# A hybrid of convolution, scan, attention and experts: the first chunk of layer 2 prepared in one go, its second keys put behind the first piece

## The chip, the cores and the metric

The kernel runs on one core of a Trainium2 chip. A core has five engines with queues of their own: PE (matmuls), ACT (functions of one operand), DVE (vector work), POOL (a second, slower vector engine) and SP (which issues DMAs here). Each works through its instructions in order and waits for semaphores. The metric is the device time of one launch in microseconds; less is better.

## What is computed

Four layers over four images of 56 x 56 positions with 128 channels. Layer 0 is neighbourhood attention, layer 1 a two-layer selective scan, layer 2 additive attention and an expert stage, layer 3 softmax attention and a second expert stage. The change lies at the start of layer 2's attention, which is, per image (3136 tokens after a layer norm, 16 hidden units):

```python
f = jnp.einsum('bih,ha->bia', x, W1[:h])
g = jnp.einsum('bjh,ha->bja', x, W1[h:])
t = jnp.tanh(f[:, :, None, :] + g[:, None, :, :] + b1)
scores = jnp.einsum('bija,a->bij', t, w2[:, 0]) + b2[0]
flag = jnp.tril(jnp.ones((n_seq, n_seq), dtype=x.dtype), -1)[None, :, :]
e = jnp.exp(scores) * flag
w = e / (jnp.sum(e, axis=-1, keepdims=True) + 1e-10)
return jnp.einsum('bij,bjh->bih', w, x)
```

Every pair of a query and an earlier key costs 16 tangents.

## The kernel before, in words

**Tiling.** A token tile has 112 tokens (`TP`), an image 28 of them (`NT`). Queries are taken in chunks of seven tiles (`WT`), 784 columns. On the 128 partitions lie eight keys (`JG`) times 16 hidden units, so a key tile has 14 groups of eight keys (`NG`). `fT` holds a chunk's query term (128 x 784; the 16 units eight times below each other), `g` the key term, one column of it for each group of eight keys.

**Pieces.** A piece is half a key tile against a chunk of queries: seven slots of up to 784 columns in one tile `th` (three buffers). In the first chunk of an image every key tile meets only the queries behind it, so the pieces of that chunk shrink: 784, 728, 672, 616, ... 56 columns for each slot; the next chunk begins at 784 again. A piece goes through four steps:
- `adds` (L1297, DVE): seven instructions, each `fT` plus one column of `g`.
- `tangents` (L1306, ACT): one tanh in place over all seven slots.
- `scores` (L1320, PE): `place` (a 0/1 matrix scaled by `w2`) sums the 16 units; four groups of columns of the array work at once. The result lies in one of two PSUM tiles `s`.
- every second piece: `weights` (L1334 or L1337, ACT exponential; on the diagonal a mask L1341 on POOL) and `weighted` (L1350, PE) with the keys' rows `xk`.

The loop over the pieces is a schedule written out by hand: DVE's adds run two pieces ahead of ACT's tangents, the exponential of a key tile comes three pieces behind, its weighted sum four. A list of small steps (`now`, `later_on`, `behind`) is dealt into the loop; from piece 2 on it holds the preparation of the next chunk.

**Preparing a chunk** (`chunk_steps`) is done in two parts, four token tiles and then three. For each part: the norm on DVE (L1221, into `xa`), transposes on PE (L1230), a copy out of PSUM on DVE (L1233, into `xT`), a memset on POOL (L1237) and eight DMAs (L1244) that bring `xa` into the order of `xk`, the key term (L1253 on PE: eight matmuls, two instructions each; L1261 on DVE adds `b1`), and the query term (L1271 on PE; L1275 on DVE copies it into `fT`). All PSUM results of it go through one bank `m`; `xa` and `xT` have one buffer each.

**The start of layer 2.** For the first chunk of the first image there is nothing to lie beside: its steps run straight behind layer 1. The weights `wf` and `wg` (L1379, L1380) and the scaling of `place` (L1381) are made on DVE after the first transposes. Only then come the adds of pieces 0 and 1 and the loop.

**The end of layer 1.** The layer norm of image 0 for layer 2 needs means and variances: 28 pairs of instructions on DVE (L1131, L1132) and a root (`rstd`, L179 to L187, with a Sqrt on ACT at L181). Image 0 has long been complete there; 20 of the pairs are put ahead of the last step of layer 1 on DVE (L920, the residual of the last image, which waits for the matmuls L904), eight and the root behind it.

Of the kernel before, what the change touches and what calls it, by code (L numbers as in the profile page):

```python
# [11 lines left out]
AF = mybir.ActivationFunctionType  # L12
ALU = mybir.AluOpType
# [5 lines left out]
B, HW, C = 4, 56, 128  # L19
S = HW * HW  # L20
P = 128
TP = 2 * HW
NT = S // TP
TC = 4
CH = TC * TP
# [30 lines left out]
AH = 16  # L56
JG = P // AH
NG = TP // JG
QW = 32

WT = 7
# [77 lines left out]
class Hybrid:  # L139
# [612 lines left out]
    def layer1(self):  # L752
# [3 lines left out]
        nc, a, tc = self.nc, self.a, self.tc  # L756
        ET = mybir.EngineType
        with ExitStack() as ctx:
            w = self.w1
            big = ctx.enter_context(tc.tile_pool(name="l1_big", bufs=1, reuse_waits="tile"))  # L760
            sm = ctx.enter_context(tc.tile_pool(name="l1_sm", bufs=2, reuse_waits="tile"))
# [6 lines left out]
            m = lambda: self.t(ps_m, [P, 512], "m")  # L768
# [7 lines left out]
            n_pairs = PAIRS * len(order)  # L776
# [147 lines left out]
            po, first, last = {}, {}, {}  # L924
            add = lambda to, at, f, *args: to.setdefault(at, []).append(lambda: f(*args))
            for j, block in enumerate(order):
                at = PAIRS * j
                if j and block[1:] == (0, 0):

                    g = self.group_norm(block[0], big, w["group"])  # L930
# [9 lines left out]
                    to = at - 2 * PAIRS  # L940
# [16 lines left out]
            g = self.first_norm  # L957
# [4 lines left out]
                turned = lambda c=c: (g.turn(c, m), g.scaled(c, g.ps))  # L962
                add(last, (-4, 2, 10, 12, PAIRS + 2, PAIRS + 10)[c - 1], turned)
            for n, step in enumerate(self.first_stats()):
                add(first if n < 20 else last, n_pairs if n < 20 else n_pairs + 10, step)
            for p in range(-4, n_pairs + PAIRS):
                if inside(p + 1):
                    in_place(p + 1)
# [170 lines left out]
    def layer2_attention(self):  # L1139
# [3 lines left out]
        nc, a, tc = self.nc, self.a, self.tc  # L1143
        ET = mybir.EngineType
        with ExitStack() as ctx:
            wp = ctx.enter_context(tc.tile_pool(name="l2_w", bufs=1, reuse_waits="tile"))
            W1, b1, w2, b2, place, later, back = self.l2

            wf = self.t(wp, [P, JG, AH], "wf")
            wg = self.t(wp, [P, 2 * P - AH], "wg")  # L1150

            big = ctx.enter_context(tc.tile_pool(name="l2_big", bufs=1, reuse_waits="tile"))
            sm = ctx.enter_context(tc.tile_pool(name="l2_sm", bufs=2, reuse_waits="tile"))
            ps_m = ctx.enter_context(tc.tile_pool(name="l2_m", bufs=1, reuse_waits="tile", space=PSUM))
            ps_h = ctx.enter_context(tc.tile_pool(name="l2_h", bufs=1, reuse_waits="tile", space=PSUM))
            ps_s = ctx.enter_context(tc.tile_pool(name="l2_s", bufs=2, reuse_waits="tile", space=PSUM))
            ps_o = ctx.enter_context(tc.tile_pool(name="l2_o", bufs=1, reuse_waits="tile", space=PSUM))
# [3 lines left out]
            m = lambda: self.t(ps_m, [P, 512], "m")  # L1161
            hold = lambda: self.t(ps_h, [P, 512], "h")
# [3 lines left out]
            im, fT, po, ps, th, es = {}, {}, {}, {}, {}, {}  # L1166
            g, xk = {}, {}
# [11 lines left out]
            def span(j, J, half=0):  # L1179

                t, n = chunks[order[j][1]]
                return max(J - t, 0) * TP + (half * TP // 2 if J >= t else 0), n * TP
# [4 lines left out]
            def image_steps(b):  # L1187

                r = im[b] = self.l2_first if b == 0 else {}
                if b == 0:  # L1190
                    return []
                x = self.X[b]

                def stats(t0):
                    if t0 == 0:
                        r["mv"] = self.t(sm, [TP, NT, 2], "ln_mv", bufs=1)
                    for t in range(t0, t0 + 2):
                        st = self.t(sm, [TP, nc.vector.BN_STATS_DIM], "ln_st", bufs=4)
                        nc.vector.bn_stats(st, x[:, t, :])
                        nc.vector.bn_aggr(r["mv"][:, t, :], st)  # L1200

                def root():
                    r["r"] = self.rstd(sm, r["mv"][:, :, 1], [TP, NT], 1e-5, "li", bufs=1)

                return [bind(stats, t) for t in range(0, NT, 2)] + [root]
# [84 lines left out]
            def adds(i):  # L1290
                j, J, half = pieces[i]
                lo, hi = span(j, J, half)
                b = order[j][0]
                th[i] = self.t(sm, [P, NG // 2, WT * TP], "th", bufs=3)
                for s, (blk, q) in enumerate(sum(rounds(half), [])):
                    at = NG * (J % WT) + NG // 2 * half + 2 * blk + (q % 2 if blk < 3 else 0)
                    nc.vector.tensor_scalar(  # L1297
                        th[i][:, s, lo:hi], fT[j][:, lo:hi], g[b, J // WT][:, at : at + 1],
                        None, op0=ALU.add,
                    )  # L1300

            def tangents(i):
                j, J, half = pieces[i]
                lo, hi = span(j, J, half)
                own = th[i][:, :, lo:hi]
                nc.scalar.activation(own, own, AF.Tanh)  # L1306
# [49 lines left out]
            def attended(j):  # L1356
# [13 lines left out]

                return [bind(copied, h) for h in range(2)], [bind(added, s) for s in range(0, n, 2)]

            run = lambda step: (step() or (lambda: None))()
            nc.gpsimd.memset(wg, 0.0)
            image_steps(0)
            start = chunk_steps(0)
            for step in start[:3]:
                run(step)
            nc.vector.tensor_copy(wf, W1[:, 0:1, :].to_broadcast([P, JG, AH]))  # L1379
            nc.vector.tensor_copy(wg[:, P - AH : P], W1[:, 1, :])  # L1380
            nc.vector.tensor_scalar(place, place, w2, None, op0=ALU.mult)  # L1381
            for step in start[3:]:
                run(step)
            weights2 = lambda: setattr(self, "w2", self.experts2_weights(self.f2_w, m))
            urgent, now, later_on, behind = [], [], [], []
            state = SimpleNamespace(held=False, after=lambda: None, dealt=0, credit=0)
            first = {}
# [3 lines left out]
            def add_ahead(i):  # L1391
                if i < len(pieces):
                    j = pieces[i][0]
                    if i == first[j] and j:
                        while now or later_on:
                            assert not state.held
                            run((now or later_on).pop(0))
                    adds(i)


            def deal():
                state.after()
                state.dealt += 1
                step = None
                if urgent and not state.held:
                    step = urgent.pop(0)
                elif now and not state.held:
                    step = now.pop(0)
                elif later_on and state.dealt % 2 and not state.held:
                    step = later_on.pop(0)  # L1410
                elif behind:
                    step = behind.pop(0)
                    state.held = step.holds
                state.after = (step and step()) or (lambda: None)
# [8 lines left out]
            def choose(b):  # L1423

                behind.extend(self.choose_steps(
                    b - 1, self.f2_pooled[:, :, b - 1], self.w2, pools, root
                ))
                if b == B - 1:
                    behind.extend(self.experts2_steps(
                        range(B - 1), self.f2_pooled, self.w2, pools, 2.5, lambda: None  # L1430
                    ))

            add_ahead(0)
            add_ahead(1)
            for i, (j, J, half) in enumerate(pieces):
                tangents(i)
                b, k = order[j]
                if half == 0 and J == 1 and k + 1 < len(chunks):
                    now += chunk_steps(j + 1)
                    if j == 0:  # L1440
                        now.append(weights2)
                if half == 0 and J == 8 and k + 1 == len(chunks) and b + 1 < B:
                    assert not behind
                    later_on += image_steps(b + 1) + chunk_steps(j + 1)
                if b and half == 0 and (k, J) == ((0, 2) if b == B - 1 else (1, 0)):
                    choose(b)
                lo, hi = span(j, J, half)
                state.credit = min(state.credit + SHARE * (hi - lo) / (WT * TP), 2)
                may = [state.credit >= n for n in (1, 2)]
                state.credit -= sum(may)  # L1450
                if may[0]:
                    deal()
                add_ahead(i + 2)
                if i >= 4 and half == 0:
                    gather(*pieces[i - 4][:2])
                scores(i)
                state.after()
                state.after = lambda: None
                if i >= 3 and half == 1:
                    weights(*pieces[i - 3][:2])  # L1460
                if may[1]:
                    deal()
            state.after()
            j, J, _ = pieces[-1]
# [742 lines left out]
```

## Time and profile before

| | us |
|---|---|
| median of 3 runs | 7028.35 (7022.07 to 7032.54) |
| profiled execution | 7027.59 |
| its span | 7025.8 |
| PE, DVE, ACT, POOL busy | 6054.1, 5763.3, 4832.9, 2849.9 |
| mean granted PE clock | 0.931 |
| last step of layer 1 on DVE (L920) starts | 2979.29 |
| first norm of layer 2 (L1221) starts | 2984.91 |
| first add (L1297) starts | 3002.85 |
| first tanh (L1306) starts | 3008.15 |
| last tanh starts | 5599.1 |

The profile shows one execution. All times in it are microseconds from the start of its span. Its views used below: the timeline (instructions of an engine in order of time; in square brackets the time that the engine stood idle ahead of one and what ended that), the groups by line, the chain of waits that ended last, and a table of busy times by stage with the granted PE clock.

### The profile page before, as it was taken

The page shows a single profiled execution, that of the slowest core. Times are in us where ns is not written, and L with a number is a line of the kernel's source. Part 1 is how long each engine was busy: PE and PEld are TensorE (multiplying, and loading weights), DVE is VectorE, ACT ScalarE, POOL GpSimd, SP SyncE. Part 2 cuts the span into 40 slices and gives each one's busy share as a digit, 9 for nine tenths or more (in the row PEclk, how much of TensorE's full clock was granted, in tenths as well). Part 3 has the DMA queues.
Part 4 walks back from the last instruction along what each step waited for, and adds up shares of the span by engine and source line. Part 5 has one row for each costly group of instructions (what it writes and reads, how often), then busy time and mean ns, then how long its engine had stood idle before and what let it go on. Part 6 is the DMA issues. An engine that isn't in the chain of part 4 may idle for free.

```text
span 7025.8 us, 101491 instructions
## 1 busy us (share of the span) xinstructions
PE 6054.1 (86%) x37386; PEld 2622.7 (37%) x37386; DVE 5763.3 (82%) x10108; ACT 4832.9 (69%) x4828; POOL 2849.9 (41%) x1921
## 2 busy tenths in 40 slices
PE   8889999999999999877777777777788799999998
PEld 7633333333233233232233323332333355555554
DVE  6879999999999999977878888888887753566665
ACT  5567667776766777589989998999899833322231
POOL 2369989998999999811010001000101100000000
PEclk9989989999999899889999999999899999999999
DMA  3057767777776777600000000000003304243433
GB/s 53 5 139 187 187 165 186 184 178 175 188 185 171 176 189 187 153 8 3 1 6 3 8 2 6 4 6 3 6 20 116 89 18 149 72 109 92 118 85 94
DMA packets 363447, 654.19 MB, mean 93 GB/s; under 512 B 95413, under 2 KB 211909, under 8 KB 362438
## 3 DMA queue, kind: packets, MB, share of 16 engines
q1 hardware_dynamic: 362949, 647.71, 36.9%
q8 instruction: 295, 4.83, 0.3%
q14 instruction: 203, 1.66, 0.1%
HBM read 536.78 MB, written 104.37 MB: 91 GB/s over the span
## 4 chain that ended last, share of the span: by engine, by line
PE 23%; ACT 12%; DVE 11%; issue 8%; POOL 1%; SPq 0%; DMA 0%; DVEq 0%; ACTq 0%; POOLq 0%
ACT th L1306 10%; PE o L1944 6%; DVE th L1297 6%; PE q L1932 5%; PE s L1320 5%; DVE X L2144 2%; PE pe L2139 2%; ACT e L1334 1%; POOL e L1341 1%; PE o L1350 1%; PE m L1478 1%; PE m L1253 1%; DVE wide L1964 1%; DVE X L1486 0%; PE m L1761 0%
## 5 line engine op out<-in xcount | busy, mean ns | idle before, releaser
L1306 ACT ACTIVATE th<-th 128x5488 f32<-128x5488 f32 (+13 forms) x560 | 2184.2, 3943 | 175.4 <-DVE th L1297 151.4
L1297 DVE TENSOR_SCALAR th<-fT,g 128x784 f32<-128x784 f32 (+13 forms) x3920 | 1868.9, 549 | 307.2 <-PE s L1320 286.5
L1320 PE MATMUL s<-th,place 128*32 128x392 f32 (+5 forms) x14112 | 1391.6, 488 | 442.2 <-ACT th L1306 439.5
L860 DVE TENSOR_TENSOR_SCAN hs<-E,u 128x896 f32<-128x896 f32 x728 | 1449.7, 2007 | 3.6 <-ACT E L844 3.6
L844 ACT ACTIVATE E<-E,rate 128x448 f32<-128x448 f32 x1456 | 886.0, 661 | 121.9 <-DMA E<-delta_dram 118.4
L865 POOL TENSOR_TENSOR hs<-hs,room 128x896 f32<-128x896 f32 x448 | 924.8, 2083 | 82.9 <-DVE hs L860 82.5
L865 POOL TENSOR_TENSOR hs<-hs,bc 128x896 f32<-128x896 f32 x448 | 926.5, 2087 | 47.3 <-DVE hs L860 45.6
L1320 PEld LDWEIGHTS s<-th,place 128*32 128x32 f32 (+1 forms) x14112 | 455.1, 111 | 1311.1 <-ACT th L1306 666.3
L1937 ACT ACTIVATE e<-q,shift 128x448 f32<-128x448 f32 (+1 forms) x511 | 322.0, 633 | 673.7 <-PE q L1932 653.4
L1341 POOL TENSOR_TENSOR e<-e,later 112x112 f32<-112x112 f32 x112 | 155.0, 1384 | 1131.4 <-ACT e L1334 676.6
L2144 DVE SCALAR_TENSOR_TENSOR X<-pe,r_gate,X 112x128 f32<-112x128 f32 x896 | 311.9, 348 | 309.6 <-PE pe L2139 273.5
L871 PE MATMUL y<-hs,sum 128*32 128x448 f32 x3584 | 499.4, 631 | 4.0 <-POOL hs L865 4.0
L1932 PE MATMUL q<-xT 128*128 128x448 f32 (+1 forms) x1022 | 501.3, 573 | 0.9 <-ACT e L1937 0.9
L1944 PE MATMUL o<-e,xk 128*128 128x448 f32 (+1 forms) x1022 | 479.2, 552 | 16.1 <-ACT oT L1909 16.1
L806 PE MATMUL u<-room,pick 32*128 32x448 f32 x1456 | 413.4, 638 | 68.5 <-DVE hs L860 66.7
L1350 PE MATMUL o<-e,xk 112*128 112x392 f32 (+5 forms) x1024 | 389.3, 500 | 91.8 <-POOL e L1341 88.2
L806 PE MATMUL u<-du,pick 32*128 32x448 f32 x1456 | 402.8, 618 | 74.2 <-DVE hs L860 72.9
L1237 POOL MEMSET xa<- 112x4 f32 (+1 forms) x32 | 55.1, 1723 | 969.9 <-PE m L1230 969.8
L853 DVE TENSOR_TENSOR u<-u,bc 128x896 f32<-128x896 f32 x364 | 391.8, 1076 | 26.1 <-PE u L806 25.8
L853 DVE TENSOR_TENSOR u<-u,room 128x896 f32<-128x896 f32 x364 | 391.8, 1076 | 22.0 <-PE u L806 21.9
L2073 POOL MEMSET lc_xa<- 112x4 f32 x28 | 3.1, 109 | 945.7 <-DVE lc_xa L2067 696.4
L848 ACT ACTIVATE u<-u 128x896 f32<-128x896 f32 x168 | 151.9, 904 | 297.3 <-PE u L797 218.1
(310 smaller groups left out, 8767.5 us busy)
## 6 DMA issues: line engine op xcount, KB each, us to landing
E<-delta_dram SPq DMA_DIRECT2D x728, 448.0 KB
V<-du_dram SPq DMA_DIRECT2D x168, 448.0 KB
wide<-in_L_ffn_weight SPq DMA_DIRECT2D x64, 1024.0 KB
r<-M SPq DMA_DIRECT2D x189, 224.0 KB
M<-wide SPq DMA_DIRECT2D x72, 392.0 KB
du_dram<-room SPq DMA_DIRECT2D x112, 112.0 KB
delta_dram<-room SPq DMA_DIRECT2D x112, 112.0 KB
du_dram<-du SPq DMA_DIRECT2D x112, 112.0 KB
```

The lines of the kernel that those rows point to most:

```text
L806: nc.tensor.matmul(halves(to)[:, k], w["pick"][own, q, :], pre[j]["du"][own, f], start=True, stop=True,)
L844: nc.scalar.activation(e, e, AF.Exp, scale=rate)
L853: eng.tensor_mul(v, v, pre[p // PAIRS]["bc"][:, 0:1].to_broadcast([P, 2, CH]))
L860: nc.vector.tensor_tensor_scan(flat, E.pop(p), V.pop(p), 0.0, op0=ALU.mult, op1=ALU.add)
L865: nc.gpsimd.tensor_mul(HS[p], HS[p], bc[:, 1:2].to_broadcast([P, 2, CH]))
L871: nc.tensor.matmul(py[j, f][r * HD : (r + 1) * HD, :], w["sum"][:, q, :], HS[p + r // 2][:, r % 2], start=False, stop=(q == QG - 1),)
L1297: nc.vector.tensor_scalar(th[i][:, s, lo:hi], fT[j][:, lo:hi], g[b, J // WT][:, at : at + 1], None, op0=ALU.add,)
L1306: nc.scalar.activation(own, own, AF.Tanh)
L1320: nc.tensor.matmul(ps[j, J][QW * blk : QW * blk + rows, h, lo:hi], place[:, off : off + rows], z[:, at + s, h * HALF + lo : h * HALF + hi] ...
L1350: nc.tensor.matmul(po[j][:, h, lo:hi], xk[b, J // WT][:, J % WT, :], e[:, h * HALF + lo : h * HALF + hi], start=(J == 0), stop=(J == t + ( ...
L1932: nc.tensor.matmul(ps[:n, :CH], of_tile(xT[b], t), xT[b][:, c * CH : (c + 1) * CH], start=True, stop=True,)
L1944: nc.tensor.matmul(po[b, c], xk[b][:n, t, :], e[:n], start=first, stop=last)
```

## The change

The first chunk is no longer prepared by `chunk_steps` but by a function of its own, `first_chunk`, with `first_keys` behind it for the memsets and DMAs:
- All seven norms follow each other on DVE, with an `xa` of its own for each part (the second in the buffer of `oT`) and an `xT` of its own (the second in a buffer of `fT`). `wf` and `wg` are made ahead of the norms, `place` is scaled behind them.
- The results go through six PSUM banks: `m` and `hold` for the transposes, the two of `o` for the queries, the two of the first `s` for the keys.
- `xT` and `fT` are copied out of PSUM by ACT instead of DVE.
- On PE the order is: transposes of both parts, keys of part 0, queries of part 0, queries of part 1. The keys of part 1 are returned as `later_keys`.
- A tanh of one column (`warm`) is issued on ACT first of all.
- The tangents of piece 0 are seven instructions, one for each slot, issued right behind its adds; `later_keys` follows, and then the adds of piece 1.
- 24 of the 28 pairs of statistics instead of 20 stand ahead of the last step of layer 1.

```diff
-                add(first if n < 20 else last, n_pairs if n < 20 else n_pairs + 10, step)
+                add(first if n < 24 else last, n_pairs if n < 24 else n_pairs + 10, step)
...
+            def first_chunk():
+
+                parts = (0, TC), (TC, WT)
+                r = im[0]
+                warm = self.t(wp, [P, 1], "warm")
+                nc.scalar.activation(warm, b1, AF.Tanh)
+                xT = [self.t(big, [P, CH], "xT"), self.t(sm, [P, WT * TP], "fT")]
+                fT[0] = self.t(sm, [P, WT * TP], "fT")
+                xk[0, 0] = self.t(big, [TP, WT, C], "xk0")
+                g[0, 0] = self.t(big, [P, WT * NG], "g0")
+                xa = [
+                    self.t(big, [TP, TC, C], "xa"),
+                    self.t(sm, [P, WT * TP], "oT", bufs=1)[:TP, : TC * C].rearrange("p (k c) -> p k c", c=C),
+                ]
+                room_q, room_k = self.t(ps_o, [P, 2, 512], "o"), self.t(ps_s, [P, 2, 512], "s")
+                nc.vector.tensor_copy(wf, W1[:, 0:1, :].to_broadcast([P, JG, AH]))
+                nc.vector.tensor_copy(wg[:, P - AH : P], W1[:, 1, :])
+                for n, (t0, t1) in enumerate(parts):
+                    ps = (m, hold)[n]()
+                    for t in range(t0, t1):
+                        nc.vector.tensor_scalar(
+                            xa[n][:, t - t0, :], self.X[0][:, t, :], r["mv"][:, t, 0:1],
+                            r["r"][:, t : t + 1], op0=ALU.subtract, op1=ALU.mult,
+                        )
+                        nc.tensor.transpose(
+                            ps[:, (t - t0) * TP : (t - t0 + 1) * TP], xa[n][:, t - t0, :],
+                            self.ident[:TP, :TP],
+                        )
+                    nc.scalar.copy(xT[n][:, : (t1 - t0) * TP], ps[:, : (t1 - t0) * TP])
+                nc.vector.tensor_scalar(place, place, w2, None, op0=ALU.mult)
+
+                def keys(n, t0, t1):
+                    ps = room_k[:, n, : (t1 - t0) * NG]
+                    by_key = xT[n][:, : (t1 - t0) * TP].rearrange("p (g j) -> p g j", j=JG)
+                    for i in range(JG):
+                        nc.tensor.matmul(
+                            ps, wg[:, P - AH - i * AH : 2 * P - AH - i * AH], by_key[:, :, i],
+                            start=(i == 0), stop=(i == JG - 1),
+                        )
+                    nc.vector.tensor_scalar(g[0, 0][:, t0 * NG : t1 * NG], ps, b1, None, op0=ALU.add)
+
+                keys(0, *parts[0])
+                for n, (t0, t1) in enumerate(parts):
+                    ps = room_q[:, n, : (t1 - t0) * TP]
+                    nc.tensor.matmul(
+                        ps, wf.rearrange("p j a -> p (j a)"), xT[n][:, : (t1 - t0) * TP],
+                        start=True, stop=True,
+                    )
+                    nc.scalar.copy(fT[0][:, t0 * TP : t1 * TP], ps)
+                return xa, parts, lambda: keys(1, *parts[1])
+
+            def first_keys(xa, parts):
+                for n, (t0, t1) in enumerate(parts):
+                    nc.gpsimd.memset(xa[n][:, : t1 - t0, C - 1 : C], 1.0)
...
-            start = chunk_steps(0)
-            for step in start[:3]:
-                run(step)
-            nc.vector.tensor_copy(wf, W1[:, 0:1, :].to_broadcast([P, JG, AH]))
-            nc.vector.tensor_copy(wg[:, P - AH : P], W1[:, 1, :])
-            nc.vector.tensor_scalar(place, place, w2, None, op0=ALU.mult)
-            for step in start[3:]:
-                run(step)
+            xa, parts, later_keys = first_chunk()
+            first_keys(xa, parts)
...
             add_ahead(0)
+            for s in range(NG // 2):
+                nc.scalar.activation(th[0][:, s, :], th[0][:, s, :], AF.Tanh)
+            later_keys()
             add_ahead(1)
             for i, (j, J, half) in enumerate(pieces):
-                tangents(i)
+                if i:
+                    tangents(i)
```

The rest of `first_keys`, left out, is the loop of eight DMAs for each part, as in `chunk_steps`.

More of the change, by code (lines that the diff above doesn't have):

```diff
@@ new lines, in first_keys @@
+            def first_keys(xa, parts):
+                for n, (t0, t1) in enumerate(parts):
+                    nc.gpsimd.memset(xa[n][:, : t1 - t0, C - 1 : C], 1.0)
+                    for blk in range(4):
+                        rows = min(QW, TP - QW * blk) // 2
+                        for half in range(2):
+                            to, of = QW * blk + rows * half, TP // 2 * half + QW // 2 * blk
+                            nc.sync.dma_start(
+                                out=xk[0, 0][to : to + rows, t0:t1], in_=xa[n][of : of + rows, : t1 - t0]
+                            )
```

## The prediction

> **What bounds the kernel now.** The per-slice part of the page first: no single engine bounds the whole. Inside layer 2's attention (about 3003 to 5600 us) the groups by line give ACT's tanh 2184.2 us and DVE's adds 1868.9 us; the stage table puts ACT at 2410 of 2592 us, so there ACT is nearly full. The chain of waits begins only at 3050.32 us, behind the place of the change, so it can't price it. I therefore read the timelines of DVE, ACT and PE from 2970 to 3055 us.
>
> DVE's timeline (start, duration, line, operands; in brackets the idle time ahead and who ended it):
>
> ```profile
> 2979.29 0.69 DVE L920 TENSOR_TENSOR X<-m,X 112x512 f32<-112x512 f32 x1 [1.43 <-PE m L904]
> ...
> 2984.91 1.11 DVE L1221 TENSOR_SCALAR xa<-X,ln_mv,ln_r 112x128 f32<-112x128 f32 x4
> ...
> 2991.23 0.28 DVE L1261 TENSOR_SCALAR g<-m,b 128x56 f32<-128x56 f32 x1 [3.66 <-PE m L1253]
> 2993.46 0.62 DVE L1275 COPY fT<-m 128x448 f32<-128x448 f32 x1 [1.96 <-PE m L1271]
> 2994.82 0.86 DVE L1221 TENSOR_SCALAR xa<-X,ln_mv,ln_r 112x128 f32<-112x128 f32 x3 [0.74 <-DMA xk<-xa]
> ...
> 3000.47 0.26 DVE L1261 TENSOR_SCALAR g<-m,b 128x42 f32<-128x42 f32 x1 [3.74 <-PE m L1253]
> 3002.31 0.51 DVE L1275 COPY fT<-m 128x336 f32<-128x336 f32 x1 [1.58 <-PE m L1271]
> 3002.85 10.77 DVE L1297 TENSOR_SCALAR th<-fT,g 128x784 f32<-128x784 f32 x21
> 3018.19 3.24 DVE L1297 TENSOR_SCALAR th<-fT,g 128x616 f32<-128x616 f32 x7 [4.58 <-PE s L1320]
> ```
>
> Two rounds of norm, transpose, keys, queries run one behind the other; all share one PSUM bank, one xT, one xa. ACT over the same stretch:
>
> ```profile
> 3006.86 1.28 ACT L1306 ACT_TABLE_LOAD   x1 [23.22 <-DVE th L1297]
> 3008.15 13.14 ACT L1306 ACTIVATE th<-th 128x5488 f32<-128x5488 f32 x3
> 3021.55 3.80 ACT L1306 ACTIVATE th<-th 128x4312 f32<-128x4312 f32 x1 [0.26 <-DVE th L1297]
> 3025.25 0.90 ACT L1334 ACTIVATE e<-s,b 112x784 f32<-112x784 f32 x1
> ```
>
> ACT, the engine that layer 2 fills, stands 23 us, then loads a table, then starts; from there it hardly stops. And by stage (busy us of PE, PEld, DVE, ACT, POOL; then the granted clock):
>
> ```profile
> 2930.00:2940.00 10.00, 10.00 (x26) 2.54 (x26) 9.56 (x7) 4.92 (x8) 8.78 (x5) 0.50 0.74 170
> 2987.50:2991.20 3.70, 3.63 (x16) 3.49 (x16) 0.06 (x1) 0.00 (x0) 0.00 (x0) 0.50 0.18 37
> 3021.55:3052.40 30.85, 28.91 (x300) 14.47 (x292) 26.43 (x87) 27.19 (x20) 4.52 (x8) 1.00 0.07 15
> ```
>
> The preparation runs at half clock; from 3021.55 PE, at full clock, is the fullest engine of the ramp. What is worth money is how early the ramp starts.
>
> **The change, part by part.** T0 = 3002.85 is the first add's start before, T the same after.
>
> *Statistics.* A pair of L1131 and L1132 takes 0.395 us. Four more fill DVE's wait of 1.43 us: 4 x 0.395 = 1.58, so the add L920 starts some 0.1 later (nobody needs image 3 here) and the root 1.58 - 0.1 = 1.48 earlier. The copies of wf and wg now stand ahead of the norms: +0.22 (starts 2987.11 to 2987.32). First norm: 2984.91 - 1.48 + 0.22 = 2983.65.
>
> *Seven norms together.* The first four transposes end 1.62 after the first norm starts (2984.91 to 2986.53): 2985.27. ACT copies 128x448 out of PSUM in 0.53 (row L886; DVE's took 0.62): xT at 2985.85. The other three transposes, in a bank of their own, end with the seventh norm (six starts of 0.277 later) at about 2986.1. First keys 2986.0 to 2989.65 (3.63, L1253 before). The scaling of place now sits on DVE behind the norms, and the seven norms go ahead of the memsets and the 16 DMAs; DVE is then idle, SP is empty, and the rows xk are first read at 3030.58, so both cost nothing. Without that cover, 16 issues at 0.94 (15.07 us) would count.
>
> *Queries directly behind.* Banks of their own, so no eviction in between: 1.77 + 1.49 (L1271's 1.86 and 1.49, less a drain of 0.1 on the first) ends at 2992.9; ACT's copy of 336 columns lies between its rows of 224 (0.345) and 448 (0.525): 0.44. T = 2993.4, 9.45 before T0. Gone from the path: the second norm with its DMA wait of 0.74, the second transposes and xT copy, and the second keys.
>
> *Second keys behind the first piece.* Their 16 matmuls, 3.64 us (row L1253), run on PE from 2992.9 to 2996.5, under DVE's seven adds (21 adds of 784, 728 and 672 columns in 10.77: 3.76, 3.5, 3.23). Their add on DVE waits at T + 3.76 = 2997.2: 0.6 us in hand, so it costs its own 0.2. Queued behind it are the second piece's adds, for which ACT waits: whatever PE is later than that margin counts in full. On PE, the first scores queue behind the keys; nobody needs those before T + 10.7.
>
> *Seven tangents and the early table.* The load of 1.28 follows the root's Sqrt (2981.9), under the norms. By the Trainium skill ("ScalarE: Activation LUTs", What ACT_TABLE_LOAD costs) a switch is 2.66 us with its drain; the trace has 3006.7 (wait over) to 3008.15, 1.45. I take 1.45; by the rule 1.2 more would be gained. The splitting itself is against the change: one instruction took 4.7, seven of 784 columns take 0.90 alone (row of that shape) and 0.80 in a row (the exponential of 784 columns at 3025.25, the next start at 3026.05): 5.6, or 0.9 more ACT work. It starts at T + 0.65 and ends at T + 6.3, while the second piece's adds are done at T + 3.76 + 0.2 + 3.5 + 0.1 = T + 7.55. So ACT still waits, and the extra 0.9 is hidden there. If seven starts cost nothing, or as much again, the end stays. Second tanh: T + 7.6, before T0 + 10.0 (3008.15 + 4.7). Gain here 9.45 + 2.4 = 11.85.
>
> *What is late next.* Fourth piece: DVE reaches it at T + 10.7, the first scores are done at about T + 7.7, so the waits of 4.58 (DVE) and 0.26 (ACT) go: the fourth tanh starts at T + 16.0 against 3021.55, 12.15 earlier. But the ramp behind it is PE's. Before, DVE ran from 3018.19 through three pieces, two norms and the xT copy, and PE's next keys started at 3028.73. After, piece 5 needs piece 2's scores (three th buffers): tanh 2 ends at T + 12.0, and PE has then been idle for over 4 us. Nearest row: 28 such matmuls after 3.14 us idle took 4.53 (3078.07); after 2.22 idle they took 2.83 (3131.48). With 4.53: T + 16.5, then 3.03 + 0.5 + 2.8 + 0.6 of DVE: keys at T + 23.4 = 3016.8, 11.9 earlier. With 2.83, ACT is the limit: T + 22.1, 13.2 earlier. I take the former, its idle time being nearer. Behind it each queue holds the same work in the same order, so the shift should last to the end: nothing later waits for a clock of its own.
>
> **Sum.** 11.9 us off the profiled execution: 7027.59 (span 7025.8 and 1.8 around it) - 11.9 = 7015.7. The median of the runs is 0.76 above the profiled one: 7016.4; I say 7016.
>
> **Rivals.**
> *PE's clock comes up early.* From 2986 to 2996.5 PE would have no gap. By the Trainium skill ("TensorE: Matmul & The Clock Gate", Part 1) some 3.4 us of sustained activity bring the full clock. Then the two queries halve (3.26 to 1.6), the keys perhaps lose 0.8, and the warm scores of piece 2 bring 1.3 more: gain 13.3 to 15.6, about 7013.5. Against it stands the first row of the stage table: 10.00 of 10.00 us busy, clock 0.50 throughout; and keys of 56 columns leave most of each 0.23 us to the weight load (PEld 3.49 of 3.63). For it: those 10 us are matmuls of 32 rows, while the queries use all 128. Row against rule, I hold to the row. Chance 0.30.
>
> *Part of it is given back in the ramp.* If the shift meets another limit before 3052 (POOL's mask, a longer cold stretch), 3 to 7 us are lost: 7019 to 7023. Against it: the same queues in the same order. Chance 0.12.
>
> *The tangents don't follow the adds.* If dependencies held for a whole tile, the seven would start at T + 3.8 and end at T + 9.4: 1.8 less, about 7018. Against it: the transpose at 2985.40 started before the four norms ended at 2986.02, so slices are tracked. Chance 0.04.
>
> *Slower.* POOL's diagonal mask L1341 took 10.51 us at 3052.33 instead of 0.42 while DVE ran 28 adds on end, and PE stood for it. DVE is ahead by one or two pieces after the change; should that make an unbroken run of adds stand beside the masks of J = 0 to 4 too, each costs about 10 us of PE and some 2 us of cold matmuls behind it. One cancels the gain; from the third on it is slower beyond what can be told from no change: -11.9 + 3 x 12 = +24, about 7052. Against it: piece 5 waits for PE as before, so DVE's lead is used up by then. Chance 0.04.
>
> **How the numbers follow.** A measurement of this kernel tells about 0.2% (14.1 us) from no change; the three runs spread over 10 us. So "faster" is below 7014.3. The forecast (0.50) lies 2 us on the near side of that line: with a scatter of some 2.5 us of a median it passes it about one time in five (0.11). Of the clock's case about two thirds pass (0.20). Together 0.31. Slower: 0.04, the rest same: 0.65. Range: 7010 (the clock's full case less scatter) to 7022 (most of the give-back).
>
> **What would show it.** First add (L1297) at about 2993.4; no L1306 table load with a wait of 23 us ahead of it, but one right behind L181's Sqrt; seven tanh of 784 columns starting about 0.65 behind the first add; second tanh at about 3001.0, fourth at 3009.4, PE's next keys at 3016.8 with clock 0.50 up to about 3010; the diagonal mask of 10.5 us near 3040.4. Wrong if the clock before 2996 is 1.00, if the second keys' add holds DVE, or if the 10.5 us mask appears once more.

## The result and the profile after

| | us |
|---|---|
| before, median of 14 runs | 7027.02 (7020.81 to 7032.54) |
| changed, median of 14 runs | 7012.48 (7004.38 to 7020.54) |
| ratio changed to before | 0.9982, 95% interval 0.9975 to 0.9990 |

The medians differ by 14.5 us; the ratio, which is estimated from all runs, stands for 12.6 us of 7027, its interval for 7.0 to 17.6. The profiled execution of the changed kernel has a span of 7002.6 us, 23.2 less than before's; but 8.6 of these are there already when layer 1 ends on PE (the last L904 matmul ends at 2970.67 instead of 2979.25). In the eight experiments below, in which PE does the same work up to there, that point lies between 2970.7 and 2983.1, so it is scatter of layer 1. I therefore measure the change by **D**, the time from the end of L904 to PE's first keys of the *next* chunk (L1253): 49.48 us before (2979.25 to 3028.73), 39.44 after (2970.67 to 3010.11). The change is worth 10.0 us there. The two ends of D on PE before:

```profile
2975.92 3.33 PE L904 MATMUL m<-ow,yg 128*112 128x128 f32 x14 [1.14 <-POOL yg L887]
...
3028.73 2.02 PE L1253 MATMUL m<-xT,wg 128*128 128x56 f32 x16 [0.75 <-DVE xT L1233]
```

In this execution the shift lasts through layer 2: its last tanh starts 2609.1 us behind L904's end (at 5579.8), before 2619.9 (at 5599.1), so 10.7 less. In the single executions of the experiments the same difference lies between 2.1 us lost and 14.2 gained, up to 9.3 away from D's. Behind the next keys an execution scatters by as much as the change is worth, so the experiments are compared by D alone.

DVE's timeline after (start, duration, line, operands, idle time ahead of it and who ended that; L1393 are the norms, L1412 the keys' add; in the experiments some lines have other numbers):

```profile
2965.43 0.21 DVE L1388 COPY wf<-W 128x128 f32<-128x128 f32 x1
...
2967.56 0.17 DVE L1389 COPY wg<-W 128x16 f32<-128x16 f32 x1 [1.65 <-POOL wg L1436]
...
2972.46 0.66 DVE L920 TENSOR_TENSOR X<-m,X 112x512 f32<-112x512 f32 x1
...
2976.47 1.11 DVE L1393 TENSOR_SCALAR xa<-X,ln_mv,ln_r 112x128 f32<-112x128 f32 x4
...
2982.47 0.28 DVE L1412 TENSOR_SCALAR g<-s,b 128x56 f32<-128x56 f32 x1 [3.96 <-PE s L1408]
2986.66 3.85 DVE L1297 TENSOR_SCALAR th<-fT,g 128x784 f32<-128x784 f32 x7 [3.92 <-ACT fT L1421]
2990.43 0.25 DVE L1412 TENSOR_SCALAR g<-s,b 128x42 f32<-128x42 f32 x1
```

The second keys' add follows the seven adds without a wait, as forecast. But the copies of wf and wg don't stand ahead of the norms: in the built program they stand among the statistics, as they need nothing of the root, and the second waits 1.65 us for POOL's memset of wg. The statistics queue behind it, so L920 starts 1.79 us behind L904's end (0.04 before). ACT after:

```profile
2965.98 0.21 ACT L1378 ACTIVATE warm<-b 128x1 f32<-128x1 f32 x1
2966.20 1.28 ACT L181 ACT_TABLE_LOAD   x1
...
2987.35 1.28 ACT L1491 ACT_TABLE_LOAD   x1 [0.73 <-DVE th L1297]
2988.65 5.34 ACT L1491 ACTIVATE th<-th 128x784 f32<-128x784 f32 x7
2994.33 12.16 ACT L1306 ACTIVATE th<-th 128x5096 f32<-128x5096 f32 x3 [0.35 <-DVE th L1297]
```

The one-column tanh was taken ahead of the Sqrt too, while the table of the layer before was still loaded: it brought no load forward, and the tangents pay 1.28 us. The second tanh still waits 0.35 us for DVE. PE after:

```profile
2967.34 3.33 PE L904 MATMUL m<-ow,yg 128*112 128x128 f32 x14 [1.14 <-POOL yg L887]
...
2978.80 3.63 PE L1408 MATMUL s<-xT,wg 128*128 128x56 f32 x16
2982.24 1.80 PE L1417 MATMUL o<-xT,wf 128*128 128x448 f32 x2
2984.66 1.49 PE L1417 MATMUL o<-fT,wf 128*128 128x336 f32 x2 [0.62 <-ACT fT L1421]
2985.95 3.48 PE L1408 MATMUL s<-fT,wg 128*128 128x42 f32 x16
2989.56 6.60 PE L1320 MATMUL s<-th,place 128*32 128x392 f32 x28
2998.84 6.52 PE L1320 MATMUL s<-th,place 128*32 128x336 f32 x56 [2.68 <-ACT th L1306]
3005.29 0.41 PE L1230 MATMUL m<-ident,xa 112*128 112x112 f32 x2
...
3010.11 2.02 PE L1253 MATMUL m<-xT,wg 128*128 128x56 f32 x16 [0.76 <-DVE xT L1233]
```

The second queries wait 0.62 us for ACT's copy of the first, though the banks differ. By stage (length, busy us of PE, PEld (the loading of weights), DVE, ACT, POOL, then the granted clock), from the first transposes through most of the first scores:

```profile
2976.90:2995.00 18.10, 17.28 (x67) 11.43 (x70) 10.23 (x25) 9.23 (x13) 0.21 (x2) 0.50 0.10 24
```

PE is busy for 17.28 of 18.10 us, and the clock stays at one half.

### The profile page after: what moved, and what is told of

The parts are those of the page before. It is cut to its first block, busy times and chain, and to the rows that moved or that the text cites. A ratio compares the mean times of both kernels' runs of the same rounds, so it can differ in the third digit from the quotient of the medians.

```text
span 7002.6 us, 101491 instructions
## 1 busy us (share of the span) xinstructions
PE 6044.5 (86%) x37386; PEld 2618.2 (37%) x37386; DVE 5761.9 (82%) x10104; ACT 4837.9 (69%) x4839; POOL 2846.4 (41%) x1921
## 3 DMA queue, kind: packets, MB, share of 16 engines
q14 instruction: 202, 1.65, 0.1%
## 4 chain that ended last, share of the span: by engine, by line
PE 23%; ACT 12%; DVE 12%; issue 8%; POOL 1%; DMA 0%; SPq 0%; DVEq 0%; ACTq 0%; POOLq 0%
ACT th L1306 10%; PE o L2004 6%; DVE th L1297 6%; PE q L1992 5%; PE s L1320 5%; PE pe L2199 2%; DVE X L2204 2%; POOL e L1341 1%; ACT e L1334 1%; PE o L1350 1%; PE m L1538 1%; DVE wide L2024 1%; PE m L1253 1%; DVE X L1546 0%; PE m L1821 0%
```

## The experiments

**Theory**: the preparation is one chain (statistics, root, norms, keys, queries, adds, second tanh, scores, DVE's steps, next keys), and whatever lengthens a link on it comes out in D in full; two links are longer than forecast, by a wait for wg and by a wait of PE for ACT. **Rivals**: those waits only cover others, so that their removal gives nothing; or ACT's own work, not the chain through DVE and PE, sets the second tanh; or PE's clock decides. Eight kernels, all measured by D, in one profiled execution each. Pieces count from 0 here (the prediction counts them from 1). Columns, in us: first norm behind L904's end; first add behind the first norm; second tanh behind the first add; next keys behind the first add; D, their sum without the third column; ratio to before with interval.

| | norm | add | tanh 2 | keys | D | ratio |
|---|---|---|---|---|---|---|
| before | 5.66 | 17.94 | 10.0 | 25.88 | 49.48 | 1 |
| changed | 5.80 | 10.19 | 7.67 | 23.45 | 39.44 | 0.9982 (0.9975 to 0.9990) |
| e1_late_weights | 4.10 | 10.14 | 7.67 | 22.39 | 36.63 | 0.9974 (0.9965 to 0.9982) |
| e2_own_bank | 5.80 | 9.21 | 7.68 | 23.47 | 38.48 | 0.9973 (0.9962 to 0.9984) |
| e3_one_tanh | 5.80 | 10.20 | 9.98 | 26.25 | 42.25 | 0.9989 (0.9982 to 0.9995) |
| e4_keys_first | 5.80 | 13.17 | 7.50 | 23.36 | 42.33 | 0.9988 (0.9981 to 0.9994) |
| e5_only_24 | 4.11 | 18.02 | 10.0 | 24.92 | 47.05 | 0.9994 (0.9985 to 1.0003) |
| e6_late_load | 5.80 | 10.20 | 7.67 | 23.46 | 39.46 | 0.9984 (0.9975 to 0.9993) |
| e8_both | 4.10 | 9.14 | 7.68 | 24.27 | 37.51 | 0.9979 (0.9970 to 0.9988) |
| e7_dense | 4.10 | 7.77 | 7.67 | 23.54 | 35.41 | 0.9977 (0.9968 to 0.9986) |

(The second tanh of before and of only 24 is worked out: the first one's start plus 4.7.) The intervals of the ratios are some 9 to 15 us wide and can't separate the last microseconds; D can. They hold D's gain (own bank's 11.0 us at the edge of 11.2 to 26.7), but all nine ratios stand for more than it, by 0.5 to 8 us. Part of that may come from the runs of before, which four experiments at a time share; the traces don't show where more would be gained.

**Late weights.** The wait among the statistics.

```diff
-                nc.vector.tensor_copy(wf, W1[:, 0:1, :].to_broadcast([P, JG, AH]))
-                nc.vector.tensor_copy(wg[:, P - AH : P], W1[:, 1, :])
                 for n, (t0, t1) in enumerate(parts):
...
+                nc.vector.tensor_copy(wf, W1[:, 0:1, :].to_broadcast([P, JG, AH]))
+                nc.vector.tensor_copy(wg[:, P - AH : P], W1[:, 1, :])
                 nc.vector.tensor_scalar(place, place, w2, None, op0=ALU.mult)
```

> The copies of wf and wg stand behind the seven norms instead of ahead of them; nothing else differs from the changed kernel. Measure for all runs: D, the time from the end of the last L904 matmul (end of layer 1 on PE) to the start of the next chunk's first keys (L1253 on PE), 49.48 us before and 39.44 after. Theory: DVE's statistics stand 1.65 us at the wg copy, which was pulled in between them and waits for POOL's memset of wg, so the last add of layer 1 (L920) starts 1.75 us behind L904's end instead of 0.04. Then here L920 starts 0.1 behind L904's end and D is 37.8. Rival: the statistics (24 pairs of 0.395 us) are simply too many to be done by then, and the wait lies beside it; D stays at 39.4.

L920 starts at 2983.19, 0.09 behind L904's end (2983.10), and the first norm 4.10 behind it. DVE's timeline of this run:

```profile
2983.19 0.66 DVE L920 TENSOR_TENSOR X<-m,X 112x512 f32<-112x512 f32 x1
...
2987.20 1.11 DVE L1391 TENSOR_SCALAR xa<-X,ln_mv,ln_r 112x128 f32<-112x128 f32 x4
```

The theory holds: 1.70 us by one move. D is 1.2 us below the forecast, because the scores of piece 1 met the full clock here (28 matmuls in 2.65 us at a clock of 1.00 after 3.29 idle; in the changed kernel, after 2.68 idle, the clock was 0.62 up to 3003.20, shortly before DVE went on, and that piece and the next together took 6.52).

**Own bank.** The wait ahead of the second queries.

```diff
-                    ps = room_q[:, n, : (t1 - t0) * TP]
+                    ps = (room_q[:, 0, : (t1 - t0) * TP], hold()[:, : (t1 - t0) * TP])[n]
```

> The queries of part 1 go into the bank of hold instead of the second bank of the tile whose first bank holds the queries of part 0. Theory: the wait of 0.62 us ahead of the second queries is one for the whole tile (PE may write its second bank only when ACT has read the first), so it goes here: second queries right behind the first, first add 0.6 us earlier behind the first norm (9.55 instead of 10.19), D 38.8. Rival: PE waits for something else (ACT's copy of xT, the evicted first queries as such), and D stays at 39.4.

PE's timeline of this run:

```profile
2984.30 1.80 PE L1417 MATMUL o<-xT,wf 128*128 128x448 f32 x2
2985.89 1.33 PE L1417 MATMUL h<-fT,wf 128*128 128x336 f32 x2
2987.01 1.94 PE L1408 MATMUL s<-fT,wg 128*128 128x42 f32 x16
```

The wait is gone, the first add comes 0.98 us earlier: 0.62, and the rest is the overlap of the two queries that became possible (the second starts 1.59 us behind the first, which takes 1.80). The two banks differed before too, so it was a wait for the whole PSUM tile. The second keys took 1.94 us instead of 3.48, at a clock of 0.97; they are hidden, so D has nothing of it.

**One tanh.** The split of piece 0.

```diff
-            for s in range(NG // 2):
-                nc.scalar.activation(th[0][:, s, :], th[0][:, s, :], AF.Tanh)
+            nc.scalar.activation(th[0], th[0], AF.Tanh)
```

> The tangents of piece 0 are one instruction again; the second keys stay behind its adds. Theory: the first tanh then starts when all seven adds are done and the table is loaded, some 5.2 us behind the first add, and ends at 9.9; the second tanh starts there instead of at 7.67 behind the first add, and the ramp follows: D about 41.8. Rival: the seven starts cost ACT what they bring, the second tanh hangs on DVE's adds anyway: D within 0.5 of 39.4.

The second tanh starts 9.98 us behind the first add, and DVE's fourth piece waits for the first scores again, as before the change (4.58 us there):

```profile
3005.00 3.24 DVE L1297 TENSOR_SCALAR th<-fT,g 128x616 f32<-128x616 f32 x7 [4.78 <-PE s L1320]
```

The split is worth 2.3 us at the second tanh and 2.8 in D; its seven instructions take 5.34 us against 4.78 for one, which stays hidden.

**Keys first.** The second keys ahead of the first piece.

```diff
+            later_keys()
             add_ahead(0)
             for s in range(NG // 2):
                 nc.scalar.activation(th[0][:, s, :], th[0][:, s, :], AF.Tanh)
-            later_keys()
```

> The second keys and their add stand ahead of the adds of piece 0 (PE's order is the same, DVE's differs by one instruction). Theory: the first add waits for the 16 key matmuls (3.5 us at half clock) behind the second queries, so it starts 3.1 us later and everything behind it too: D about 42.4. Rival: ACT and PE have slack there (PE stands 2.68 us ahead of piece 1's scores), and less than 1 us comes through: D under 40.5.

DVE's timeline of this run:

```profile
2990.32 0.26 DVE L1412 TENSOR_SCALAR g<-s,b 128x42 f32<-128x42 f32 x1 [6.72 <-PE s L1408]
2990.49 13.91 DVE L1297 TENSOR_SCALAR th<-fT,g 128x784 f32<-128x784 f32 x28
```

The first add starts 2.98 us later, D is 2.89 longer: the theory. Putting them behind is worth that much, and PE's slack ahead of piece 1 doesn't absorb it.

**Only the 24 pairs**, on the kernel before.

```diff
-                add(first if n < 20 else last, n_pairs if n < 20 else n_pairs + 10, step)
+                add(first if n < 24 else last, n_pairs if n < 24 else n_pairs + 10, step)
```

> The kernel before with one edit of the change alone: 24 of the 28 pairs of statistics ahead of the last step of layer 1. Here the copies of wf and wg stay behind the norms, so nothing is pulled in between the pairs. Theory: the first norm starts 4.2 us behind L904's end instead of 5.66 and everything behind it shifts by as much: D (end of L904 to the next chunk's first keys, 49.48 before) about 48.0; 1.5 us of the time, which is below what the time can tell. Rival: the shift is lost in the later waits of the preparation (the second norm waits for a DMA): D 49.0 or more.

The first norm moves from 5.66 to 4.11 behind L904's end: the 1.5 us are there when nothing is pulled in between. Of D's 2.4 us the other 0.96 lie behind the first add, where the first 28 scores took 4.10 us at a clock of 0.69 (before, the clock was 0.55 from 3012.98 to 3018.10); I put that down to the clock's turn, not to the edit; no run tells the two apart.

**Late load.** The tanh that should load the table reads the root.

```diff
-                nc.scalar.activation(warm, b1, AF.Tanh)
+                nc.scalar.activation(warm[:TP], r["r"][:, 0:1], AF.Tanh)
```

> The changed kernel with the one-column tanh reading the root of the statistics instead of b1, so that ACT can't take it ahead of the Sqrt; its result isn't used anywhere in either kernel. Theory: the table load moves from 0.7 us behind the first add to the time of the norms and the seven tangents of piece 0 start 1.35 us earlier, but the second tanh waits for DVE's adds anyway: ACT's wait ahead of it grows from 0.35 to about 1.6 us and D stays 39.4 (0.3 less at most). Rival: ACT's lateness counts, and D is 38.1.

ACT's timeline of this run:

```profile
2983.36 1.28 ACT L1378 ACT_TABLE_LOAD   x1
...
2995.53 5.34 ACT L1491 ACTIVATE th<-th 128x784 f32<-128x784 f32 x7 [0.74 <-DVE th L1297]
3002.49 12.15 ACT L1306 ACTIVATE th<-th 128x5096 f32<-128x5096 f32 x3 [1.62 <-DVE th L1297]
```

The load went to where it was meant, the tangents began 1.3 us earlier behind the first add, and all of it turned into a longer wait for DVE: D 39.46. With the tangents split, ACT's table load doesn't set the start of the second tanh; DVE's fourteen adds do.

**Both.** The edits of the first two and of the late load together.

> The changed kernel with three mends together: wf and wg behind the norms, the second queries in a bank of another tile, the table load behind the Sqrt. Theory: the gains add up, since they lie one behind the other on the same path: norms 1.7 us earlier behind L904's end, first add 1.0 earlier behind the first norm, the load nothing: D about 36.8, and 35.6 if piece 1's scores should find the full clock as with the late weights alone. Rival: with both, DVE's adds run into the limit of ACT or of the scores, and D stays at or above 37.5.

The two moves add up as far as the first add (4.10 + 9.14, against 5.80 + 10.19: 2.75 us). Behind it they don't: D came out 0.7 over the forecast and at its rival's bound of 37.5. The limit was the scores, one of the two that the rival names, and not ACT, whose second tanh stands at 7.68 as ever. The scores of pieces 1 and 2 ran at a clock of 0.50 from 2996.16 to 3001.30 and DVE waited for them:

```profile
2996.16 7.87 PE L1320 MATMUL s<-th,place 128*32 128x336 f32 x56 [3.67 <-ACT th L1306]
3001.36 3.04 DVE L1297 TENSOR_SCALAR th<-fT,g 128x560 f32<-128x560 f32 x7 [2.78 <-PE s L1320]
```

**Dense.** With late weights and own bank, PE is kept busy between layer 1 and the first transposes; three matmuls are added whose result isn't used (the other edits are left out here).

```diff
+                hot = hold()
+                for i in range(3):
+                    nc.tensor.matmul(
+                        hot, self.X[B - 1][:, NT - 1, :],
+                        self.X[B - 1][:, NT - TC :, :].rearrange("p t c -> p (t c)"),
+                        start=True, stop=True,
+                    )
```

> Late weights and own bank as in the run of both (without the late load), and three matmuls of 112 rows by 512 columns on PE between the end of layer 1 and the first transposes; their result is read by nobody, they only keep PE busy (6.4 us at half clock, about 5 if the clock comes up within them). Theory of the clock: [...]the keys of part 0 then take 2.0 instead of 3.63 and the queries 1.6 instead of 3.3, and even with transposes that are late by 1 to 2 us D is about 34 to 35.5. Rival: the norms' gap or the thin matmuls of the keys (a clock of 0.50 through all of them in both kernels) let the clock fall again: the keys take 3.6, and D is 37 to 39 because the transposes are late.

By stage (columns as above): the added matmuls and the transposes; most of the keys' first half; the rest of the keys and the queries; the second keys:

```profile
2977.80:2983.30 5.50, 4.53 (x13) 2.02 (x13) 4.86 (x24) 0.76 (x2) 0.12 (x1) 1.00 0.00 0
2983.30:2984.40 1.10, 1.10 (x11) 1.09 (x10) 0.04 (x1) 0.44 (x1) 0.10 (x1) 1.00 0.13 30
2984.40:2987.60 3.20, 3.20 (x12) 2.38 (x11) 0.28 (x1) 0.09 (x1) 0.00 (x0) 0.52 0.20 42
2988.00:2990.00 2.00, 2.00 (x18) 1.85 (x16) 1.14 (x3) 0.93 (x3) 0.00 (x0) 1.00 0.16 33
```

Each theory had half of it. The clock was up at the added matmuls (2.84 us instead of the 6.4 that I had estimated for half clock, so the transposes weren't late) and stayed up through half of the keys, which took 2.53 us; then it fell while PE was busy without a gap, and came back at about 2988, at the end of the queries. The first add came 1.4 us earlier behind the first norm than in the run of both (7.77 against 9.14). D of 35.41 is the shortest measured, 14.1 us below before; its ratio can't be told from the changed kernel's.

So the chain sets D up to the first add, and the rival of the clock holds in part behind it: in the kernels with the split tangents and the second keys behind the first piece, the next keys lie between 22.39 and 24.27 us behind the first add, by the clock that the scores of pieces 1 and 2 met.

## Why the prediction was right

The forecast was 7016 us, the measured median is 7012.48; the mechanism was the forecast one, the first chunk's chain made shorter. Part of the agreement is luck. The median fell by 14.5 us, more than the 11.9 of the forecast, while D fell by less, 10.0; by the median alone the rival with an early clock (gain 13.3 to 15.6, about 7013.5) would look better, and only the trace, with its clock of 0.50, speaks against it. Term by term (T is the start of the first add, as in the prediction):

- **Statistics and the first norm**: forecast 1.26 us earlier behind L904's end, measured 0.14 later. This is the term that failed most. "The copies of wf and wg now stand ahead of the norms: +0.22" took the order of the source for that of the queue; they were pulled among the statistics, and what waits behind the wg copy there is the whole path. With late weights the term is 1.56, and the edit to 24 pairs alone gives 1.55.
- **Norms to keys**: forecast 2.35 us from the first norm to the first keys and 3.63 for them; measured 2.33 and 3.63. The 16 DMA issues are hidden, as forecast; their 15.07 us before hold SP's wait between the two parts, as eight take 6.34 and eight 5.36.
- **"Banks of their own, so no eviction in between"**: wrong by 0.62 us, since both lie in one tile. First add 10.19 behind the first norm instead of 9.75; with a tile of its own it comes at 9.21, below the forecast, as the sum also left out that the matmuls overlap. The two errors partly cancel.
- **Second keys**: hidden, as forecast; 0.25 us on DVE. In front they cost 2.9.
- **The table load behind Sqrt**: did not happen. The forecast had priced it as part of what is hidden, and the late load shows why nothing was missed: the second tanh stands at T + 7.67 with the load early or late (forecast T + 7.6). In the changed kernel ACT was done only 0.35 us before that. DVE's 21 adds, which the forecast split into 3.76, 3.5 and 3.23, add up to 10.77 in its row, not to 10.49.
- **Ramp**: next keys at T + 23.45 (forecast 23.4). The first scores ended at T + 9.5, not T + 7.7, so PE was idle for 2.68 us, not over 4, ahead of piece 1's; these were slow all the same. That was not certain: in the seven kernels with such a pause, of 2.68 to 4.57 us, they were slow six times, and fast after 3.29 us with late weights, where the next keys came at T + 22.39 (the forecast's other case has T + 22.1).
- **D**: forecast 11.9 less, measured 10.0; the 1.9 are the 1.4 of the statistics and the 0.4 of the queries. Both gains lie in the interval of 7.0 to 17.6, so the time alone would not have shown the error. What the medians' 14.5 us have beyond 10.0 is not accounted for by the change; the late load, with the same D, gives 11.2 us by its ratio (4.9 to 17.6).
- **Rivals**: the clock stayed at one half through the preparation, so its rival failed here. The row of 10.00 us busy at 0.50 was the better guide than the rule of the Trainium skill ("TensorE: Matmul & The Clock Gate", Part 1: some 3.4 us of sustained activity), taken by busy time, as 17.28 of 18.10 us busy left the clock at 0.50. (The matmuls of that row are 128*32 in the view: weights of 128 rows and 32 columns, not "32 rows".) The tangents followed the adds slice by slice, as forecast. The diagonal mask of 10.51 us came at T + 47.05, where it was forecast, and the change added none. But it isn't the only one of its kind: in layer 2 eight masks take 9.9 to 10.5 us, before as after, the second of them in the next chunk:

```profile
3033.71 10.51 POOL L1341 TENSOR_TENSOR e<-e,later 112x112 f32<-112x112 f32 x1 [3.92 <-ACT e L1337]
...
3154.69 10.51 POOL L1341 TENSOR_TENSOR e<-e,later 112x112 f32<-112x112 f32 x1 [1.90 <-ACT e L1337]
```

## What to carry to other kernels

A copy that is ready early is cheap only where the queue lets it stand: read the order of the built queues, and ask of each instruction that could be pulled forward what it waits for and who stands behind it (here 0.17 us of work held a path for 1.65). A helper that should load something early needs a dependency that puts it there, and two halves of one tile may wait for each other although their banks differ. When a change of a few microseconds drowns in the scatter of the whole, measure it between two fixed instructions on the path.

## What was not expected of the hardware

Busy time on PE doesn't tell what the granted clock will do. In the run of both mends, PE was busy without a gap in every stage from 2976 to 2989 (and for 3.49 of the next 3.50 us), with a clock of 0.50 up to 2989; with the own bank alone, the same gapless sequence had a clock of 0.97 after 8 us. One stage of each, the run of both first:

```profile
2986.70:2989.00 2.30, 2.30 (x14) 1.05 (x16) 2.30 (x7) 2.30 (x4) 0.00 (x0) 0.50 0.13 29
2987.00:2989.00 2.00, 1.96 (x17) 1.80 (x15) 1.27 (x3) 1.01 (x2) 0.00 (x0) 0.97 0.15 37
```

In the dense run the clock fell at about 2984.5 under key matmuls of 56 columns, which spend most of their time on loading weights (PEld 1.09 of 1.10 us). In the changed kernel it was 1.00 from 2996 to 2998 and 0.50 again from 3000 to 3002, behind an idle time of only 2.68 us. Idle times of 3.29 us (late weights) and 3.30 us (own bank, dense) were followed by fast and by slow scores. What the clock answers to beyond this, the runs don't show.
